# A 32-partition shift copied by ScalarE instead of loaded, and evictions shared 8 to 7, in the mixing stage of a long convolution

## The chip, the cores and the metric

The kernel runs on one core of one Trainium2 chip, in one launch. The metric is the device time of that launch in microseconds (us), as the median of several runs.

## The reference

The input `x` is (4, 512, 512, 16) in float32. Two layers are applied, each as a residual on a group-normalised input:

```python
x = x + _L0_conv_ref(_gn(x), h0, numerators, denumerator)   # long convolution through FFTs
x = x + _L1_conv_ref(_gn(x), kernel, bias, radius)          # 3x3 cosine-similarity convolution
```

Layer 0 builds a 512 x 512 impulse response for each of the 16 x 16 channel pairs, as a quotient of two small polynomials in the frequency plane, and convolves every channel with it:

```python
X = jnp.fft.rfft2(x, s=(2 * l1, 2 * l2), axes=(-3, -2))
Y = jnp.einsum('...hwi,ijhw->...hwj', X, H_full)
y = jnp.fft.irfft2(Y, s=(2 * l1, 2 * l2), axes=(-3, -2))[..., :l1, :l2, :]
```

Layer 1 divides a 3 x 3 convolution by norms of the input and the kernel, takes an arccosine, and gates with two tanh factors. The change is in layer 0, where `X` is multiplied by `H_full` and summed over the 16 input channels.

## The kernel before

The launch has four phases: the filter (`filter_phase`), the transform of the input along one image axis (`forward_phase`), the mixing (`conv_phase`), and the transform back with the whole of layer 1 (`last_phase`). They hand data on through tensors in HBM: `g_d` (filter), `x_d` (input), `y_d` (result).

`conv_phase` works through 513 rows, one for each frequency along the first axis. For one row, everything along the other axis is transformed, multiplied and transformed back in blocks. The steps of a row are spread over several turns of the loop, so that in turn n:

- `mix` multiplies row n. For each of 128 frequencies it takes the weights `gh` (128 values of contraction by 32) and the input `xe` and writes the PSUM tile `pm`, 32 partitions for each quarter of the frequencies. `pm` is evicted to `yf`, once in each of the four parts k = 0 to 3 of a turn. `pm` has two buffers.
- `g_part` transforms the filter of row n+1 (PSUM tiles `pg0` and `pg1`, three buffers in all) and evicts it to `gh`, two evictions in each part. The first `mix` of a row needs the whole `gh` of that row.
- `over_q` transposes `yf` of row n-1 into `pz`; ScalarE copies half of it to `zq`, and five VectorE operations form `z` from `zq` and `pz`.
- `x_part` (k=0) transforms the input of row n+2 into `px`, evicted in two halves to `xe[:, 0]`. `x_late` then multiplies this by phases on GpSimd (four `xu`, then two operations on `xl`), and GpSimd stores `xe[:, 0]` and `xl` to `xf_d`.
- `half_shift` and `load_xe` complete `xe`. `xe` holds eight copies t = 0 to 7 of the row, each shifted by 16 t partitions, where what runs out at the end is taken from `xl`. t = 4, a shift by 64 partitions, is made by two ScalarE copies of 64 partitions; the six others are loaded from `xf_d` by SP in the next turn.
- `turn_x` (k=2) makes the transform matrix of a row (`turn` on ScalarE, `dfs_n` on VectorE).
- `over_g` (k=2) transforms `z` of row n-2 back into `py`, evicted to `yo` and stored by GpSimd.

`px`, `pz` and `py` share three PSUM buffers. Fifteen evictions in a row go through one helper, `evict`: every third goes to VectorE (in the settled rows four `gh` and one `xe`), the rest to ScalarE (four `gh`, four `yf`, one `xe`, one `yo`). Its lines are 728 (VectorE) and 730 (ScalarE).

Each engine works through its instructions in one fixed order. That order is made when the program is built: a scheduler takes instructions from the Python program by priority as they become ready by its own model, so an instruction can stand ahead of others that come before it in the text. In the settled rows ScalarE's order is: `yf`, `gh`, `zq` of k=0; `xe`; half shift 0; `yf` of k=1; `turn`; `gh`, `zq` of k=1; half shift 1; `yf`, `gh`, `zq` of k=2; `yo`; `yf`, `gh`, `zq` of k=3. VectorE's is: `gh`, `z` of k=0; `xe`; `dfs_n`; `gh`, `z` of k=1, of k=2, of k=3.

Of the kernel before, what the change touches and what calls it, by code (L numbers as in the profile page):

```python
# [46 lines left out]
P = 128  # L47
N = 512
B = 4
C = 16  # L50
# [6 lines left out]
XF = F * 2 * B  # L57
XP = XF + 128
# [138 lines left out]
def dram(t, row, offset, *dims):  # L197

    pitch = t.shape[1]
    lead = [[pitch, t.shape[0]]] if row is None else []  # L200
    return bass.AP(tensor=t.tensor, offset=t.offset + (row or 0) * pitch + offset,
                   ap=lead + [list(d) for d in dims])
# [494 lines left out]
def conv_phase(tc, cst, g_d, x_d, y_d):  # L697
    nc = tc.nc
    with ExitStack() as ctx:
# [20 lines left out]
        rows = [(0, 0, 0), (0, 0, 1)] + [(n // P, n % P, None) for n in range(1, N)]  # L720
        n_rows = len(rows)
        state = {}
        flip = [0]

        def evict(dst, src):
            flip[0] += 1
            if flip[0] % 3 == 0:
                nc.vector.tensor_copy(dst, src)  # L728
            else:
                nc.scalar.copy(dst, src)  # L730

        def load_g(n):
            rc, r, plane = rows[n]
            g = io.tile([P, C, 8 * C], F32, name="g")
            t, w = g.rearrange("p j x -> p (j x)"), C * 8 * C
            if plane is None:
                nc.sync.dma_start(out=t, in_=dram(g_d[rc], r, 0, [w, P], [1, w]))
            else:
                for to, at in ((0, (0, 96)[plane]), (64, (64, 32)[plane])):
                    nc.sync.dma_start(out=t[to : to + 32], in_=dram(g_d[rc], r, at * w, [w, 32], [1, w]))  # L740
                    nc.gpsimd.memset(t[to + 32 : to + 64], 0.0)
            state["g", n] = g

        def load_x(n):
            rc, r, plane = rows[n]
            x = io.tile([P, B, 8 * C], F32, name="x")
            t, w = x.rearrange("p b x -> p (b x)"), B * 8 * C
            if plane is None:
                nc.sync.dma_start(out=t, in_=dram(x_d[rc], r, 0, [w, P], [1, w]))
            else:  # L750
                nc.gpsimd.memset(t[S:], 0.0)
                nc.sync.dma_start(out=t[:S], in_=dram(x_d[rc], r, plane * S * w, [w, S], [1, w]))
            state["x", n] = x
# [16 lines left out]
        def x_part(n, b):  # L770

            if b == 0:

                state["xe", n] = xep.tile([P, 8, F, 2, 2, 2], F32, name="xe")
            if b % 2 == 0:
                state["px"] = ps_f.tile([P, 2, F, 2], F32, name="px", tag="full")
            px = state["px"]
            nc.tensor.matmul(px[:, b % 2].rearrange("p f c -> p (f c)"), state["x", n][:, b],
                             state["dfs", n], start=True, stop=True)
            if b % 2:  # L780
                evict(state["xe", n][:, 0, :, b // 2], px.rearrange("p k f c -> p f c k"))
            if b == B - 1:
                del state["x", n], state["dfs", n]

# [22 lines left out]
        def half_shift(n, half):  # L807

            dst, src = ((slice(0, 64), state["xe", n][64:, 0]), (slice(64, P), state["xl"][:64]))[half]
            nc.scalar.copy(state["xe", n][dst, 4].rearrange("p f h c k -> p (f h c k)"),  # L810
                           src.rearrange("p f h c k -> p (f h c k)"))

        def load_xe(n):
            src = xf_d[n % 4]
            for t in (1, 5):
                nc.sync.dma_start(
                    out=state["xe", n][:, t : t + 3].rearrange("p t f h c k -> p t (f h c k)"),
                    in_=bass.AP(tensor=src.tensor, offset=src.offset + t * C * XP,
                                ap=[[XP, P], [C * XP, 3], [1, XF]]),
                )  # L820

        def g_part(n, j):


            if j % 4 == 0:
                state["pg"] = [ps_g.tile([P, 4, F], F32, name=f"pg{c}", tag="pg") for c in range(2)]
            g, pg = state["g", n], state["pg"]
            for c in range(2):
                half = slice(64 * c, 64 * c + 64)
                nc.tensor.matmul(pg[c][:, j % 4], g[half, j], dg[half], start=True, stop=True)  # L830
            if j == 3:
                state["gh", n] = ghp.tile([P, F, 2, C], F32, name="gh")
            if j % 4 == 3:
                for c in range(2):
                    evict(state["gh", n][:, :, c, j - 3 : j + 1], pg[c].rearrange("p j f -> p f j"))
            if j == C - 1:
                del state["g", n]

        def mix(n, g):

            if g % 8 == 0:
                state["pm"] = ps_m.tile([P, 8, 8, 2 * B], F32, name="pm")
            xe, gh, pm = state["xe", n], state["gh", n], state["pm"]
            for q in range(4):
                f = g + 32 * q
                nc.tensor.matmul(  # L846
                    pm[32 * q : 32 * q + 32, g % 8], gh[:, f].rearrange("p c j -> p (c j)"),
                    xe[:, :, f].rearrange("p t h c k -> p t (h c k)"), start=True, stop=True,
                )
            if g == 7:  # L850

                state["y", n] = yp.tile([P, 16, 32, 4], F32, name="yf")
            if g % 8 == 7:
                evict(state["y", n][:, :, g - 7 : g + 1].rearrange("p t g x -> p g t x"),
                      pm.rearrange("p g t (h x) -> p g (t h) x", h=2))
            if g == 31:
                del state["xe", n], state["gh", n]

# [30 lines left out]
        def over_g(n, k):  # L889

            rc, r, plane = rows[n]
            if k == 0:
                state["py"] = ps_f.tile([P, 2, 2, 8, C], F32, name="py", tag="full")
            z, d, py = state["z", n], state["zd", n], state["py"]
            odd, c2 = k // 2, k % 2
            for half in range(2):
                s0 = 2 * half + odd
                if s0 % 2 == 0:
                    zs = z[:, :, s0 + c2]
                elif s0 == 1:  # L900
                    zs = (d[:, :, 0], z[:, :, 5])[c2]
                else:
                    zs = (z[:, :, 4], d[:, :, 1])[c2]
                nc.tensor.matmul(
                    py[64 * half : 64 * half + 64, odd], ig[:, s0, c2],
                    zs.rearrange("p (t h) j -> p h t j", h=2),
                    start=(c2 == 0), stop=(c2 == 1),
                )
            if k < 3:
                return  # L910
            del state["z", n], state["zd", n]
            yo = yop.tile([P, 4 * P], F32, name="yo")
            evict(yo.rearrange("p (x j t) -> p x j t", x=4, j=C), py.rearrange("p o h t j -> p (o h) j t"))
            if plane is None:
                nc.gpsimd.dma_start(out=dram(y_d[rc], r, 0, [4 * P, P], [1, 4 * P]), in_=yo)  # L915
            else:
                for half in range(2):
                    nc.gpsimd.dma_start(
                        out=dram(y_d[rc], r, (64 * half + 32 * plane) * 4 * P, [4 * P, 32], [1, 4 * P]),
                        in_=yo[64 * half : 64 * half + 32],  # L920
                    )

        def step(n):


            def row(k):
                return 0 <= n + k < n_rows

            if row(3):
                load_x(n + 3)  # L930
            if row(2):
                load_g(n + 2)
            if row(1):
                load_xe(n + 1)
            for k in range(4):
                if row(0):
                    for g in range(8):
                        mix(n, 8 * k + g)
                if row(1):
                    for j in range(4):  # L940
                        g_part(n + 1, 4 * k + j)
                if row(-1):
                    for t in range(4):
                        over_q(n - 1, 4 * k + t)
                if row(2) and k == 0:
                    for m in range(B):
                        x_part(n + 2, m)
                    x_late(n + 2)
                if row(2) and k >= 2:
                    half_shift(n + 2, k - 2)  # L950
                if row(3) and k == 2:
                    turn_x(n + 3)
                if row(-2) and k == 2:
                    for m in range(4):
                        over_g(n - 2, m)
# [482 lines left out]
```

## Time and profile before

| | |
|---|---|
| median of 3 runs | 16582.36 us (16561.65 to 16588.23) |
| the profiled execution | 16601.06 us |
| its span, first to last instruction | 16599.1 us |
| TensorE clock granted, mean | 0.973 |
| rows of the mixing phase | 513, from 4767.9 to 13720.4 us by the last operation on `xl` |
| HBM traffic over the span | 272 GB/s; in the mixing phase about 325 |
| eviction of 128 x 512 on ScalarE, on VectorE | 592 ns (`yf`), 688 ns (`gh`) |
| half shift, 64 x 1024 | 1044 and 1051 ns |

The profile shows one execution. PE is TensorE, PEld its weight loads, DVE is VectorE, ACT ScalarE, POOL GpSimd, SP the engine that issues most of the transfers. A line such as `L730 ACT COPY yf<-pm` names the line of the kernel, the engine, the operation, and the tile written and read. In the views of waits, "A <- B: total, times, longest" says that instruction A stood idle until B ended, in us. In a timeline the first two columns are start and duration in us, and the brackets hold the idle time before it and what ended it. "issue" is idle time for which the profile shows no cause. A line of the table of windows has the length of the window, then busy time of PE, PEld, DVE, ACT and POOL, the granted clock, the share of time that the DMA engines were busy, and GB/s.

### The profile page before, as it was taken

To read this page: it belongs to the slowest core of one execution; us is meant where nothing else is said; L and a number is where in the kernel's file an instruction comes from. 1 tells how busy PE (TensorE), PEld (TensorE's weight loads), DVE (VectorE), ACT (ScalarE), POOL (GpSimd) and SP (SyncE) were. 2 spreads that over 40 slices of the span, in tenths; PEclk is the share of its full clock that TensorE was granted. 3 is DMA by queue.
4 is the path that set the end of the run, shared out by engine and by line. 5 is a ranking of instruction groups with operands and counts; after the bars stand their busy time and mean duration, and the time that the engine had idled before them with its cause. 6 is when DMAs were issued, how large, how long until landed. Compare 5 with 4: busy or idle time off the path is not lost. (4 is left out here: it accounts for less than half of the span.)

```text
span 16599.1 us, 545650 instructions
## 1 busy us (share of the span) xinstructions
PE 15057.2 (91%) x232588; PEld 11240.5 (68%) x232588; DVE 10596.9 (64%) x22299; ACT 9042.9 (54%) x18799; POOL 10362.7 (62%) x10669
## 2 busy tenths in 40 slices
PE   7999999998988899889899989898888888988888
PEld 5555555554557777777777777777777777767777
DVE  8999999993545555555555555555555552357877
ACT  5666666663345555555555555555555551027888
POOL 7777777772346666666666666666666660237766
PEclk7999999999999999999999999999999999989999
DMA  4888888878878888888888888888888886885531
GB/s 134 233 235 236 232 238 235 240 226 257 253 262 327 321 328 326 326 326 323 326 328 320 328 325 329 325 323 327 319 325 328 321 324 236 309 289 167 165 108 69
DMA packets 2914698, 4543.40 MB, mean 274 GB/s; under 512 B 126114, under 2 KB 2094460, under 8 KB 2801422
## 3 DMA queue, kind: packets, MB, share of 16 engines
q1 hardware_dynamic: 2703070, 3836.37, 67.4%
q0 software_dynamic: 172336, 605.00, 9.4%
q10 hardware_dynamic: 36864, 67.13, 1.2%
q8 instruction: 1833, 30.03, 0.7%
q14 instruction: 595, 4.87, 0.1%
HBM read 3030.71 MB, written 1477.31 MB: 272 GB/s over the span
## 5 line engine op out<-in xcount | busy, mean ns | idle before, releaser
L830 PE MATMUL pg<-c_dg,g 64*128 64x128 f32 x32832 | 2851.6, 290 | 372.2 <-ACT gh L730 220.5
L846 PE MATMUL pm<-xe,gh 128*32 128x64 f32 x131328 | 2370.2, 222 | 486.0 <-issue 234.5
L830 PEld LDWEIGHTS pg<-c_dg,g 64*128 64x128 f32 x32832 | 2293.3, 189 | 716.2 <-ACT gh L730 278.1
L846 PEld LDWEIGHTS pm<-xe,gh 128*32 128x32 f32 x131328 | 1998.2, 110 | 1072.6 <-issue 838.6
L875 DVE TENSOR_TENSOR z<-zq,pz 128x256 f32<-128x256 f32 x2052 | 859.4, 419 | 2695.4 <-ACT zq L874 2641.7
L728 DVE COPY gh<-pg 128x512 f32<-128x512 f32 x2046 | 1408.3, 688 | 1148.2 <-PE pg L830 1144.1
L450 PE MATMUL pt<-ev_in,c_todd 128*128 128x512 f32 x4096 | 1927.3, 609 | 109.0 <-ACT u L338 83.4
L799 POOL TENSOR_TENSOR xu<-xe,c_late 128x256 f32<-128x256 f32 x2052 | 1392.2, 702 | 845.6 <-ACT xe L730 826.7
L507 DVE RECIPROCAL dn<-dn 128x256 f32<-128x256 f32 x1024 | 1716.9, 1716 | 0.0
L730 ACT COPY yf<-pm 128x512 f32<-128x512 f32 x2046 | 1211.9, 592 | 901.5 <-PE pm L846 887.9
L382 POOL TENSOR_TENSOR sp<-m,dn 128x512 f32<-128x512 f32 x1024 | 1301.1, 1272 | 615.0 <-DVE dn L507 528.8
L810 ACT COPY xe<-xl 64x1024 f32<-64x1024 f32 x513 | 539.1, 1051 | 1892.1 <-POOL xl L801 1892.1
L450 PEld LDWEIGHTS pt<-ev_in,c_todd 128*128 128x128 f32 x4096 | 728.6, 190 | 1021.8 <-issue 704.3
L730 ACT COPY gh<-pg 128x512 f32<-128x512 f32 x2058 | 1201.2, 584 | 356.7 <-PE pg L830 355.1
L867 PE MATMUL pz<-c_ident,yf 128*128 128x128 f32 x8208 | 1365.6, 289 | 27.1 <-issue 14.1
L398 PEld LDWEIGHTS pg<-c_dinv,sp 64*128 64x128 f32 x16384 | 1004.5, 196 | 464.6 <-ACT sp L387 210.8
L409 ACT COPY st<-pg 128x256 f32<-128x256 f32 x2048 | 617.2, 391 | 1281.2 <-PE pg L398 1281.2
L801 POOL TENSOR_TENSOR xl<-xl,xu 128x1024 f32<-128x1024 f32 x513 | 1210.0, 2359 | 40.2
L398 PE MATMUL pg<-c_dinv,sp 64*128 64x128 f32 x16384 | 1106.7, 287 | 70.4 <-ACT sp L387 47.4
L1281 PE MATMUL pc<-l_band,xn 128*128 128x160 f32 (+2 forms) x6144 | 1078.0, 334 | 50.7 <-DVE e_o L1336 50.4
L883 POOL TENSOR_TENSOR zd<-z 128x512 f32<-128x512 f32 x513 | 653.6, 1274 | 742.4 <-DVE z L875 742.3
L915 POOL DMA_DIRECT2D y_d<-yo x511 | 296.5, 580 | 1305.0 <-ACT yo L730 1279.1
(211 smaller groups left out, 30874.7 us busy)
## 6 DMA issues: line engine op xcount, KB each, us to landing
xe<-xf_d SPq DMA_DIRECT2D x1026, 1536.0 KB
g<-g_d SPq DMA_DIRECT2D x511, 1024.0 KB
g_d<-st SPq DMA_DIRECT2D x256, 1024.0 KB
ev_in<-g_d SPq DMA_DIRECT2D x1024, 256.0 KB
g_d<-ot SPq DMA_DIRECT2D x1024, 256.0 KB
xf_d<-xe POOLq DMA_DIRECT2D x513, 448.0 KB, 8.2
xf_d<-xl POOLq DMA_DIRECT2D x513, 448.0 KB, 5.5
x_d<-xo SPq DMA_DIRECT2D x128, 1024.0 KB
```

The source lines that it names most:

```text
L382: nc.gpsimd.tensor_mul(w["sp"], w["m"], bc(w["dn"], 2, [P, 2, 2, P]))
L398: nc.tensor.matmul(pg[u][:, n, k].rearrange("p a x -> p (a x)"), w["sp"][q, k, c, :], dinv[q, 2 * kp + k, c, :], start=(c == 0), stop=(c = ...
L450: nc.tensor.matmul(pt, todd[:, c, kc, hh * P : hh * P + P], ev[:, kc, c], start=(kc == 0), stop=(kc == 1),)
L507: nc.vector.reciprocal(w["dn"], w["dn"])
L728: nc.vector.tensor_copy(dst, src)
L730: nc.scalar.copy(dst, src)
L799: nc.gpsimd.tensor_mul(u[:, :, h, c], xe[:, :, h, 1 - c], bc(late[:, 1 + c], 2, [P, F, 2]))
L801: nc.gpsimd.tensor_add(xl.rearrange("p f h c k -> p (f h c k)"), xl.rearrange("p f h c k -> p (f h c k)"), u.rearrange("p f h c k -> p (f ...
L830: nc.tensor.matmul(pg[c][:, j % 4], g[half, j], dg[half], start=True, stop=True)
L846: nc.tensor.matmul(pm[32 * q : 32 * q + 32, g % 8], gh[:, f].rearrange("p c j -> p (c j)"), xe[:, :, f].rearrange("p t h c k -> p t (h c k ...
L867: nc.tensor.transpose(pz[:, t % 4].rearrange("p v q x -> p (v q x)"), y[:, at].rearrange("p g x -> p (g x)"), ident)
L1281: nc.tensor.matmul(pc[:, lo:hi, :].rearrange("p w j -> p (w j)"), xns[q][:, h * P + dh : h * P + dh + P], bands[dh][:, o : o + hi - lo, :] ...
```

## The change

Three edits, all in `conv_phase`:

- Copy t = 2, a shift by 32 partitions, is made by four ScalarE copies of 32 partitions (`quarter_shift`): quarter 0 in part k=0, quarters 1 and 2 in k=1, quarter 3, which reads `xl`, in k=3 of the program's text.
- `load_xe` loads five copies: t = 1 and 3 in one transfer, 5 to 7 in the other.
- `evict` is told the engine: VectorE gets the second half of `xe`, `gh` of `pg1`, `yf` of k=1 and k=3, and `yo` (8 in a row); ScalarE gets 7.

```diff
-        flip = [0]
-
-        def evict(dst, src):
-            flip[0] += 1
-            if flip[0] % 3 == 0:
+
+        def evict(dst, src, vector):
+            if vector:
                 nc.vector.tensor_copy(dst, src)
             else:
                 nc.scalar.copy(dst, src)
...
-                evict(state["xe", n][:, 0, :, b // 2], px.rearrange("p k f c -> p f c k"))
+                evict(state["xe", n][:, 0, :, b // 2], px.rearrange("p k f c -> p f c k"), b == 3)
...
+        def quarter_shift(n, q):
+
+            src = state["xl"][:32] if q == 3 else state["xe", n][32 * q + 32 : 32 * q + 64, 0]
+            nc.scalar.copy(state["xe", n][32 * q : 32 * q + 32, 2].rearrange("p f h c k -> p (f h c k)"),
+                           src.rearrange("p f h c k -> p (f h c k)"))
+
         def load_xe(n):
             src = xf_d[n % 4]
-            for t in (1, 5):
+            for t in (slice(1, 4, 2), slice(5, 8)):
+                of = range(8)[t]
                 nc.sync.dma_start(
-                    out=state["xe", n][:, t : t + 3].rearrange("p t f h c k -> p t (f h c k)"),
-                    in_=bass.AP(tensor=src.tensor, offset=src.offset + t * C * XP,
-                                ap=[[XP, P], [C * XP, 3], [1, XF]]),
+                    out=state["xe", n][:, t].rearrange("p t f h c k -> p t (f h c k)"),
+                    in_=bass.AP(tensor=src.tensor, offset=src.offset + of[0] * C * XP,
+                                ap=[[XP, P], [of.step * C * XP, len(of)], [1, XF]]),
                 )
...
-                    evict(state["gh", n][:, :, c, j - 3 : j + 1], pg[c].rearrange("p j f -> p f j"))
+                    evict(state["gh", n][:, :, c, j - 3 : j + 1], pg[c].rearrange("p j f -> p f j"), c == 1)
...
-                      pm.rearrange("p g t (h x) -> p g (t h) x", h=2))
+                      pm.rearrange("p g t (h x) -> p g (t h) x", h=2), g % 16 == 15)
...
-            evict(yo.rearrange("p (x j t) -> p x j t", x=4, j=C), py.rearrange("p o h t j -> p (o h) j t"))
+            evict(yo.rearrange("p (x j t) -> p x j t", x=4, j=C), py.rearrange("p o h t j -> p (o h) j t"), True)
...
-                if row(2) and k >= 2:
-                    half_shift(n + 2, k - 2)
+                if row(2):
+                    for q in ([0], [1, 2], [], [3])[k]:
+                        quarter_shift(n + 2, q)
+                    if k >= 2:
+                        half_shift(n + 2, k - 2)
```

In the built program ScalarE's order in a settled row is: `yf`, `gh`, `zq` of k=0; `xe`; quarters 0, 1, 2; `gh`, `zq` of k=1; half shift 0; `yf` of k=2; quarter 3; `gh`, `zq` of k=2; half shift 1; `turn`; `gh`, `zq` of k=3. VectorE's is: `gh`, `z` of k=0; `xe`; `dfs_n`; `yf` of k=1; `gh`, `z` of k=1; `gh`, `z` of k=2; `yo`; `yf` of k=3; `gh`, `z` of k=3. On TensorE the first matmul into `pg0` and the first into `pg1` of the next row stand ahead of the first `mix` of a row; before, only the one into `pg0` did. On SP the two loads of `xe` come one after the other, then `g`, then `x`; before, `g` stood between the two.

## The prediction

> **What bounds the kernel now.** I read the page first, for the shares of the engines.
>
> ```profile
> PE 15057.2 (91%) x232588; PEld 11240.5 (68%) x232588; DVE 10596.9 (64%) x22299; ACT 9042.9 (54%) x18799; POOL 10362.7 (62%) x10669
> ```
>
> No engine is full over the whole span, so I went to the stage that is changed. The view of line 801 (the last step of the turned copy `xl`, once in each row) dates it: 513 rows, and (13720.4 - 4767.9) / 512 = 17.485 us a row. It also shows who waits for `xl`.
>
> ```profile
> L801 POOL TENSOR_TENSOR xl<-xl,xu x513: 2337/2360/2380, 4767.9 to 13720.4; 128x1024 f32<-128x1024 f32 x171
> ...
>   ACT xe L810: 1892.1, 513
> ```
>
> ScalarE stands 1892 / 513 = 3.7 us in every row before the half shift that reads `xl`. From the spacing of these 513 starts: 210 rows take 16.86 to 16.94 us, the median is 17.05, the tail runs to 23. Next the waits of the stage, from 4820 to 13700 us:
>
> ```profile
> DVE z L875 <- ACT zq L874: 2617.2, 1556, 6.7
> ACT xe L810 <- POOL xl L801: 1866.4, 507, 6.5
> ...
> PE pm L846 <- issue: 232.7, 259, 3.2
> PE pg L830 <- ACT gh L730: 214.5, 238, 3.8
> PE pg L830 <- issue: 144.7, 96, 2.9
> PE pm L846 <- DMA xe<-xf_d: 82.2, 73, 3.0
> ```
>
> TensorE's waits are small and spread; ScalarE and VectorE show the long regular ones. So I took one quiet row (`pm` starts at 7056.77 and again at 7073.83) from the timelines of ScalarE, VectorE and TensorE:
>
> ```profile
> 7064.96 0.38 ACT L874 COPY zq<-pz 128x256 f32<-128x256 f32 x1
> 7069.08 1.06 ACT L810 COPY xe<-xl 64x1024 f32<-64x1024 f32 x1 [3.75 <-POOL xl L801]
> 7070.16 0.59 ACT L730 COPY yf<-pm 128x512 f32<-128x512 f32 x1
> 7070.64 0.59 ACT L730 COPY gh<-pg 128x512 f32<-128x512 f32 x1
> 7071.12 0.39 ACT L874 COPY zq<-pz 128x256 f32<-128x256 f32 x1
> ```
>
> ```profile
> 7071.54 0.42 DVE L875 TENSOR_TENSOR z<-zq,pz 128x256 f32<-128x256 f32 x1 [3.98 <-ACT zq L874]
> ...
> 7073.05 0.68 DVE L728 COPY gh<-pg 128x512 f32<-128x512 f32 x1
> ```
>
> ```profile
> 7071.28 1.16 PE L830 MATMUL pg<-c_dg,g 64*128 64x128 f32 x14 [1.10 <-ACT gh L730]
> ...
> 7073.83 1.10 PE L846 MATMUL pm<-xe,gh 128*32 128x64 f32 x64 [0.39 <-ACT zq L874]
> ```
>
> The row is a loop of latencies. Counted from `pm`: `px` starts at 2.61, its evictions let GpSimd start `xu` at 4.34, `xl` ends at 12.27, the half shift ends at 13.4, then come `yf`, `gh` and `zq` on ScalarE, the five VectorE operations on `z`, and only behind them VectorE's last `gh`, which ends at 7073.73; `pm` of the next row starts 0.10 later. That wait is labelled `zq`, but `zq` had ended at 7073.48; `gh` is the last thing that `pm` needs. TensorE's own work in the row is 17.06 - 1.10 - 0.39 = 15.57 us.
>
> DMA is the near second: in the same row
>
> ```profile
> 7056.70:7073.80 17.10, 15.57 (x360) 12.55 (x360) 9.57 (x27) 9.25 (x17) 11.29 (x11) 1.00 0.89 333
> ```
>
> 333 GB/s at a share of 0.89, and 82 us of TensorE's waits are for `xe` loads.
>
> [...]`yf`, whose matmuls ended at 7065.02, sat behind the half shift until 7070.16. So the order of instructions on each engine is what must be costed. [...]the 64-partition half shifts took 1044 and 1051, so a 32-partition copy is taken at 1.04 us. [...]the quiet rows here stay at 333 to 336.
>
> **The change, part by part**, per row, with the order that the changed program has on each engine.
>
> 1. Loads. `xe` by five shifts, 2 + 3, instead of 3 + 3: 2560 KB for 3072. The row's traffic falls from 5504 KB (5.64 MB: `xe` 3072, `g` 1024, `x` 256, stores 896 + 256) to 4992 KB (5.11 MB), at 335 GB/s from 16.8 to 15.3 us. SP now issues both `xe` loads ahead of `g`; `g` lands later by the second `xe` load (1.57 MB, about 5 us), but is wanted only at the end of the row; `x` stays last. This gives back the waits for `xe`: 82 / 513 = 0.16 us a row, and no more, since the clean row does not end on a load.
>
> 2. Four quarter copies on ScalarE, 4 x 1.04 = +4.2 us; three evictions leave it (2 `yf`, 1 `yo`, 0.59 each, -1.8). ScalarE's work goes from 9.25 to about 11.6 us. Quarters 0 to 2 follow the `xe` eviction: they wait for VectorE's `xe` (5.5), run to about 8.6, and hold back `gh` and `zq` of k=1 and the first half shift to about 10.4 and `yf` of k=2 to 10.9. They hide in the 3.75 us that ScalarE idled: 1.2 us are left before `xl` ends. Without that cover each would cost 0.95 us.
>
> 3. Quarter 3 takes the half shift's place as the first reader of `xl`: same moment, same 1.04 us. Behind it come `gh` and `zq` of k=2, then the second half shift, the turn, and `gh`, `zq` of k=3. `yf` of k=2 is now ahead of the wait: -0.48 us on the chain (7070.16 to 7070.64 is the step between queued copies).
>
> 4. VectorE gets `yo` and two `yf`, loses none: 3 x 0.69 us more, 9.6 to 11.6 us. But in its queue `yo` and `yf` of k=3 stand between the operations on `z` of k=2 and the last `gh`. Those operations wait for the late `zq`; so both evictions, ready long before, run after it and ahead of the `gh` that `pm` needs. Step between queued VectorE copies: 0.60 us (7055.99 to 7056.59). +1.20 on the chain. The third, `yf` of k=1, runs at about 6.0, ahead of its waits: nothing.
>
> 5. On TensorE both first `pg` matmuls of the next row now precede `pm`, where one did. 12 instructions rather than 14 lie between `pm` and `pz`, at 1.08 / 14 = 0.078 us: -0.16. They wait for ScalarE's `gh` of k=3, done at about 16.1, before VectorE's at 17.4: nothing.
>
> 6. GpSimd: same order, same steps. Its start depends on ScalarE's `xe` eviction, which still comes before the quarters; `y_d` now waits for VectorE's `yo`, at 16.2, ahead of any use.
>
> Sum for a clean row: 16.90 - 0.16 - 0.48 + 1.20 = 17.46 us.
>
> Then the tail. TensorE is also interrupted by itself ("issue": 232.7 + 144.7 + 28 for `py` + 14 for `pz` = 420 us, 0.82 a row), partly absorbed by its slack. I took 506 rows of TensorE's timeline: row length less waits for other engines is TensorE's own time (mean 16.6, one row in ten over 18.4). The larger of this and of the chain (moved by a late `px`), averaged over the rows, is 17.34 for a chain of 16.90; with 0.16 for late loads this gives 17.50, against 17.485 measured. For a chain of 17.46 it is 17.82, without late loads. So (17.82 - 17.485) x 513 = +172 us. The profiled execution took 16601 (span 16599) and would take about 16773; the three runs' median is 19 us lower, so **16754 us**.
>
> Unknowns, both ends: interruptions may shrink with lighter DMA traffic (all gone: 17.46, -13 us) or, falling before `px` where no slack absorbs them, stay in full (17.46 + 0.43 = 17.89, +208). The chain may be 0.16 shorter (17.30: 17.68, +100) or longer (base 17.06 rather than 16.90, 17.62: 17.96, +244). I take the middle.
>
> **Rivals.**
> - Faster: the loads set the row. For it: 333 GB/s, rows that end on `xe` loads, and the changed kernel moves 9% less. If loads were the only limit, the row could fall to TensorE's 15.57 plus its interruptions 0.82 = 16.4: -1.09 x 513 = -560 us, 16020. It decides if VectorE's last `gh` ends before the loads land, that is if the chain grows by less than nothing. Against: quiet rows end 0.10 us after that `gh`, and only 73 of 513 rows name a load. 8%.
> - No change: the chain grows, but the interruptions nearly vanish with the traffic; 17.46 to 17.55, 16570 to 16615. Nothing shows that they come from traffic: in one disturbed row (7003.5 to 7023) the granted clock was 0.91. 9%.
> - Slower still: ScalarE's queue, now with 1.2 us before `xl`, fills, and the quarters push the chain. From 1.45 us per quarter on it decides; with a chain longer by 0.5 and the tail in full it is 17.46 + 0.5 + 0.4: +450 us, 17030.[...] 8%.
> - The change does not do what it says: excluded, the built program has 2 + 3 shifts and 8 to 7 evictions in each row.
>
> **The numbers.** Likeliest (75%): +70 to +290, 16650 to 16870, at 16754. The range for 8 in 10 takes in most of the no-change case below and the edge of the slower one: 16590 to 16880. A measurement here can tell about 0.2%, 33 us. Faster by more: the loads' 8% and 3 of the no-change case's 9, 11%. Within: the other 6, and 2 of the likeliest, 8%. Slower: 73 + 8 = 81%.
>
> **What would show it.** Right: `pm` of the next row waits about 1.5 to 2 us, ending 0.1 us after VectorE's `gh`, which follows `yo` and `yf` at steps of 0.60; ScalarE's wait for `xl` at about 1.2 us in front of a 32-partition copy of 1.04; waits for `xe` loads near zero at about 290 GB/s; quiet rows at 17.46. Wrong: quiet rows under 17.0, or `pm` released by a load or by ScalarE; or ScalarE no longer idle before `xl`.

## The result and the profile after

The changed kernel takes 16753.72 us (median of 4 runs, 16742.82 to 16783.95) where the kernel before takes 16585.29 (4 runs, 16561.65 to 16590.23). The ratio is 1.0108, with a 95% interval of 1.0093 to 1.0122: slower by 168 us. The forecast was 16754.

The profiled execution took 16752.71 us, its span is 16750.6, and the mean granted clock is 0.97 as before. First the page's line of engine shares, after the change:

```profile
PE 15075.3 (90%) x232588; PEld 11194.9 (67%) x232588; DVE 11532.3 (69%) x23838; ACT 10422.9 (62%) x19312; POOL 10361.8 (62%) x10669
```

ScalarE and VectorE have more to do, by 1380 and 935 us. No engine is full. Then the view of the last step of `xl`, whose line is now 799:

```profile
L799 POOL TENSOR_TENSOR xl<-xl,xu x513: 2339/2367/2460, 4765.5 to 13865.1; 128x1024 f32<-128x1024 f32 x171
...
  ACT xe L814: 460.4, 485
```

A row takes (13865.1 - 4765.5) / 512 = 17.773 us, 0.288 more than before; times 513 that is 148 of the span's 151 us. So the loss lies in the mixing phase, and in every row of it. ScalarE now waits for `xl` 460 us in all instead of 1892, and the reader is the 32-partition copy. The waits of the phase, from 4820 to 13850 us, say who waits now (total, times, longest):

```profile
DVE z L880 <- ACT zq L879: 2168.9, 1567, 5.0
...
PE pm L851 <- issue: 474.8, 406, 4.0
ACT xe L814 <- POOL xl L799: 452.8, 480, 3.7
...
PE pm L851 <- DVE gh L726: 278.9, 370, 1.3
...
PE pg L835 <- issue: 146.8, 120, 3.0
```

TensorE's waits for `xe` loads are gone from the list. In their place stand two things: `pm` waits for VectorE's `gh` in 370 rows, and TensorE's idle time without a cause in this view ("issue") has grown. Summed over `pm`, `pg`, `py`, `pz` and `px` it is 688 us, 1.35 a row, where it was 0.83. I call these stretches interruptions of TensorE.

One quiet row shows the queues: `pm` starts at 7064.08 and again at 7081.45. Its lines from the timelines of ScalarE, VectorE and TensorE (start, duration, idle time before and what ended it):

```profile
7073.15 0.38 ACT L879 COPY zq<-pz 128x256 f32<-128x256 f32 x1
...
7074.51 0.57 ACT L728 COPY yf<-pm 128x512 f32<-128x512 f32 x1
7076.05 1.05 ACT L814 COPY xe<-xl 32x1024 f32<-32x1024 f32 x1 [0.97 <-POOL xl L799]
7077.12 0.58 ACT L728 COPY gh<-pg 128x512 f32<-128x512 f32 x1
7077.60 0.38 ACT L879 COPY zq<-pz 128x256 f32<-128x256 f32 x1
```

```profile
7078.01 0.42 DVE L880 TENSOR_TENSOR z<-zq,pz 128x256 f32<-128x256 f32 x1 [2.26 <-ACT zq L879]
...
7079.52 0.68 DVE L726 COPY yo<-py 128x512 f32<-128x512 f32 x1
7080.12 0.68 DVE L726 COPY yf<-pm 128x512 f32<-128x512 f32 x1
7080.72 0.68 DVE L726 COPY gh<-pg 128x512 f32<-128x512 f32 x1
```

```profile
7064.08 1.10 PE L851 MATMUL pm<-xe,gh 128*32 128x64 f32 x64 [0.86 <-DVE gh L726]
...
7066.48 1.89 PE L776 MATMUL px<-dfs_n,x 128*128 128x256 f32 x8
...
7078.27 0.42 PE L851 MATMUL pm<-xe,gh 128*32 128x64 f32 x13 [1.52 <-issue]
...
7081.45 1.10 PE L851 MATMUL pm<-xe,gh 128*32 128x64 f32 x64 [0.51 <-DVE gh L726]
```

The chain reads from top to bottom: ScalarE stands 0.97 us for `xl`; quarter 3, `gh` and `zq` follow at once; `zq` lets VectorE form `z`; behind that come `yo` and `yf`, at steps of 0.60, and only then the `gh` that `pm` needs. It ends at 7081.40, `pm` starts at 7081.45. TensorE was interrupted for 1.52 us in this row, and still waited 0.51 us for `gh` at its end: the row takes 17.37, so the slack took the interruption up. Of 512 rows, 332 take 17.3 to 17.4 us. The table of windows shows DMA at a share of 0.79 and 290 GB/s from 5000 to 13500 us, where it was 0.87 and 325.

### The profile page after: what moved, and what is told of

It is laid out like the page before. It is cut to its first block, busy times and chain, and to the rows that moved or that the text cites. A ratio compares the mean times of both kernels' runs of the same rounds, so it can differ in the third digit from the quotient of the medians.

```text
span 16750.6 us, 547682 instructions
## 1 busy us (share of the span) xinstructions
PE 15075.3 (90%) x232588; PEld 11194.9 (67%) x232588; DVE 11532.3 (69%) x23838; ACT 10422.9 (62%) x19312; POOL 10361.8 (62%) x10669
## 5 line engine op out<-in xcount | busy, mean ns | idle before, releaser
L851 PE MATMUL pm<-xe,gh 128*32 128x64 f32 x131328 | 2414.7, 222 | 766.4 <-issue 482.3
L835 PE MATMUL pg<-c_dg,g 64*128 64x128 f32 x32832 | 2783.1, 292 | 224.6 <-issue 150.7
L835 PEld LDWEIGHTS pg<-c_dg,g 64*128 64x128 f32 x32832 | 2220.7, 189 | 573.1 <-issue 241.4
L814 ACT COPY xe<-xe 32x1024 f32<-32x1024 f32 x1539 | 1611.6, 1047 | 717.4 <-DVE xe L726 705.2
L728 ACT COPY yf<-pm 128x512 f32<-128x512 f32 x1026 | 595.1, 580 | 1016.2 <-PE pm L851 1015.9
L909 PE MATMUL py<-z,c_ig 128*64 128x256 f32 x6156 | 1068.9, 409 | 31.1 <-issue 28.1
```

The costliest lines, as they stand in the source:

```text
L814: nc.scalar.copy(state["xe", n][32 * q : 32 * q + 32, 2].rearrange("p f h c k -> p (f h c k)"), src.rearrange("p f h c k -> p (f h c k)"))
L851: nc.tensor.matmul(pm[32 * q : 32 * q + 32, g % 8], gh[:, f].rearrange("p c j -> p (c j)"), xe[:, :, f].rearrange("p t h c k -> p t (h c k ...
```

## The experiments

My theory: in a quiet row the order of instructions on ScalarE and VectorE sets the time (the loop through `xl`), and what is over it comes from interruptions of TensorE. The rivals: the loads of `xe` set the row; or the copies do, by filling ScalarE. Every kernel was measured against the kernel before on the same chip. "Quiet" is the commonest row length, to about 0.02; the mean is the spacing of all 513 `xl` starts; "idle" is TensorE's idle time of cause "issue" per row.

| | ratio to before, 95% interval | median, us | mean row | quiet row | idle |
|---|---|---|---|---|---|
| before | 1 | 16585 | 17.49 | 16.90 | 0.83 |
| changed kernel | 1.0108 (1.0093 to 1.0122) | 16754 | 17.77 | 17.33 | 1.35 |
| e1, sharing alone | 1.0218 (1.0201 to 1.0236) | 16955 | 18.19 | 17.82 | 0.96 |
| e2, shift alone | 1.0149 (1.0131 to 1.0167) | 16845 | 17.90 | 17.17 | 1.48 |
| e3, one load less | 1.0044 (1.0033 to 1.0054) | 16665 | 17.61 | 16.89 | 1.40 |
| e4, `yo` back to ScalarE | 1.0093 (1.0073 to 1.0113) | 16752 | 17.79 | 16.88 | 1.63 |
| e5, no `xe` loads | 0.9852 (0.9838 to 0.9867) | 16343 | 16.98 | 16.95 | 0.29 |
| e6, order of loads | 1.0004 (0.9995 to 1.0013) | 16599 | 17.46 | 16.90 | 0.88 |
| e7, copies of `xl` last | 0.9848 (0.9826 to 0.9871) | 16328 | 16.93 | 15.73 | 1.13 |
| e8, half shift 1 last | 1.0002 (0.9993 to 1.001) | 16590 | 17.41 | spread | 0.89 |
| e9, e3 with loads late | 1.1207 (1.1189 to 1.1226) | 18576 | 21.3 | | 0.21 |
| e10, e7 with loads late | 1.1212 (1.1196 to 1.1229) | 18596 | 21.4 | | 0.26 |

**e1: the sharing alone.** The changed kernel with six loads and the two half shifts of before.

```diff
-                if row(2):
-                    for q in ([0], [1, 2], [], [3])[k]:
-                        quarter_shift(n + 2, q)
-                    if k >= 2:
-                        half_shift(n + 2, k - 2)
+                if row(2) and k >= 2:
+                    half_shift(n + 2, k - 2)
...
-            for t in (slice(1, 4, 2), slice(5, 8)):
+            for t in (1, 5):
```

> Eviction sharing alone: 8 on VectorE and 7 on ScalarE as in the changed kernel, with six shifts loaded and two half shifts as before. Chain theory: the half shift still waits for xl, with yf, gh and zq of k=2 behind it; VectorE has yo and yf of k=3 between z of k=2 and the last gh, 2 x 0.60 us more. Quiet rows 16.90 + 1.20 = 18.1 (within 0.15), mean row near 18.3, so 16585 + 0.8 x 513 = about 17000. Rival, the loads set the row: traffic is that of before, so the time is that of before within 40 us.

Measured: 16954.85 us, and a quiet row of 17.82. Against the changed kernel that is 0.49 more. What differs on the chain is `yf` of k=2, which here still stands behind the wait for `xl`; the prediction priced that at 0.48. Against before, 0.92 more, and I had expected 1.20 for the two evictions on VectorE. By the times of the changed kernel's quiet row, 0.21 of the difference is the earlier `px` (2.40 us after `pm` here too) and 0.05 the earlier start of `pm` behind `gh`; I had left both out.

**e2: the shift alone.** Quarter copies and five loads, with evictions by every third as before.

```diff
+        def quarter_shift(n, q):
+            src = state["xl"][:32] if q == 3 else state["xe", n][32 * q + 32 : 32 * q + 64, 0]
...
-            for t in (1, 5):
+            for t in (slice(1, 4, 2), slice(5, 8)):
...
-                if row(2) and k >= 2:
-                    half_shift(n + 2, k - 2)
+                if row(2):
+                    for q in ([0], [1, 2], [], [3])[k]:
+                        quarter_shift(n + 2, q)
+                    if k >= 2:
+                        half_shift(n + 2, k - 2)
```

> Quarter copies and five loads alone, evictions as before (every third on VectorE). Chain theory: quarter 3 waits for xl, then gh, zq of k=2, half shift 1, turn, yo, yf and gh of k=3 all on ScalarE; that gh ends about 17.1 after pm and releases the next pm. Quiet rows 17.15, ended by ScalarE and not by VectorE, mean 17.6: about +50 us on before, 16640. Rival, the loads set the row: 9 percent less traffic, up to 560 us less, 16020.

Measured: 16844.84 us. The quiet row was 17.17, as expected, and it ended on ScalarE's `gh`; but the mean row is 17.90, and the idle time 1.48 a row. The mechanism of the quiet row held, the forecast of the tail failed: I had let the interruptions stay as they were. The two parts do not add up: 370 us and 260 us alone, 168 us together. In a quiet row each relieves what the other loads: the new sharing takes three evictions from ScalarE, which the quarters fill, and the quarters put `yf` of k=2 ahead of the wait for `xl`.

**e3: one load less, and nothing in its place.** The kernel before, without the load of copy t = 2; three fixed `xe` buffers hold zeros there. So it leaves out a seventh of the shifted copies that are not t = 0.

```diff
+                if n < 3:
+                    fixed[n] = xep.tile([P, 8, F, 2, 2, 2], F32, name=f"xe{n}")
+                    nc.gpsimd.memset(fixed[n][:, 2], 0.0)
+                state["xe", n] = fixed[n % 3]
...
-            for t in (1, 5):
+            for t in (slice(1, 4, 2), slice(5, 8)):
```

> The kernel before with copy t=2 neither loaded nor copied (filled with zeros once, in three fixed buffers of xe, so the output leaves this copy out). Nothing else differs on ScalarE and VectorE; SP issues g after both xe loads. Chain theory: quiet rows stay at 16.9; only the waits for xe loads go, 0.16 us a row: -80 us, 16500. Rival, the loads set the row: down to 16.4 a row, -560 us, 16020. Halfway (-250 or more) would mean that traffic costs more than the waits named after it.

Measured: 16665.39 us over 12 runs, slower by 0.44%. The quiet row stayed at 16.89, so the loads do not set it. But less traffic, at no price on any engine, made the program slower: the idle time of TensorE rose from 0.83 to 1.40 a row. This was the largest surprise, and it says that my tail was wrong in its cause.

**e4: `yo` back to ScalarE.**

```diff
-            evict(yo.rearrange("p (x j t) -> p x j t", x=4, j=C), py.rearrange("p o h t j -> p (o h) j t"), True)
+            evict(yo.rearrange("p (x j t) -> p x j t", x=4, j=C), py.rearrange("p o h t j -> p (o h) j t"), False)
```

> The changed kernel with the eviction of yo back on ScalarE, where it stands after the turn and ahead of gh of k=3. Chain theory: one step of 0.60 less ahead of VectorE's last gh: quiet rows 17.35 - 0.60 = 16.75, mean 17.3, -250 us on the changed kernel: 16500, 85 below before. Rival, ScalarE or VectorE is full (their busy time sets the row): moving 0.6 us from one to the other changes nothing beyond 50 us: 16750. Loads: traffic as in the changed kernel, 16750.

Measured: 16751.71 us, no better, although the quiet row fell by 0.45, to 16.88. It did not fall by the whole step of 0.60, because `yo` on ScalarE stands ahead of `gh` of k=3, and the first matmul into `pg1` waits for that. From e4's timelines of ScalarE and TensorE:

```profile
7067.45 0.57 ACT L728 COPY yo<-py 128x512 f32<-128x512 f32 x1
7067.91 0.59 ACT L728 COPY gh<-pg 128x512 f32<-128x512 f32 x1
```

```profile
7068.55 0.48 PE L835 MATMUL pg<-c_dg,g 64*128 64x128 f32 x2 [0.67 <-ACT gh L728]
```

And the gain of the quiet rows was taken by idle time: 1.63 a row. A shorter chain leaves less slack for interruptions to hide in; that they also grew is not explained by it.

**e5: no loads of `xe` at all.** The kernel before; the six copies hold zeros, written once.

```diff
+                    nc.gpsimd.memset(fixed[n][:, 1:4], 0.0)
+                    nc.gpsimd.memset(fixed[n][:, 5:], 0.0)
...
-            if row(1):
-                load_xe(n + 1)
```

> The kernel before without any load of xe (the six copies are filled with zeros once, so the output leaves them out); stores, g and x as before: 2432 KB a row instead of 5504. The question is TensorE's idle time without a named cause (0.82 us a row before, 1.41 in the kernel with one load less). Theory F, it is instructions of TensorE fetched late because their transfers stand among the bursts of loads: it falls under 0.3 us a row, quiet rows stay at 16.9 by the chain, mean near 17.1: -200 us, 16380. Rival C, the clock or power limit interrupts TensorE: it stays at 0.8 or more and the mean at 17.4: 16540.

Measured: 16342.84 us. The waits of e5, from 4850 to 13500 us:

```profile
PE pm L851 <- DVE gh L729: 204.2, 471, 0.4
...
PE pm L851 <- issue: 126.2, 149, 1.4
```

`pm` waits for VectorE's `gh` in nearly every row, rows take 16.95 (95% under 17.04), and the idle time falls to 0.29 a row. Of the two theories put down before the run, that of late instructions had named under 0.3 and that of the clock 0.8 or more. DMA moves 149 GB/s there instead of 325. Two things follow. The chain of queues alone gives 16.9 us, with or without loads. And nearly all that a row takes above it comes with the traffic of the `xe` loads: as waits for them, or as interruptions of TensorE.

**e6: the order of the loads.** The kernel before, with both `xe` loads ahead of `g` on SP, as in the changed kernel. It asks whether that order makes the interruptions.

```diff
+        order = InOrder(tc, nc.sync)
...
-            if row(2):
-                load_g(n + 2)
-            if row(1):
-                load_xe(n + 1)
+            with order:
+                if row(1):
+                    load_xe(n + 1)
+                if row(2):
+                    load_g(n + 2)
```

> The kernel before with six shifts loaded as before, but both loads of xe issued ahead of g on SP, as the changed kernel does. Traffic, ScalarE and VectorE as before. If the order of the loads makes the longer interruptions of the kernel with one load less: 1.2 us or more a row without cause, mean 17.6, 16650. If their start in the row does (the store of xl lands earlier with less traffic, which this kernel does not change): 0.8 to 0.9, 16585 within 40.

Measured: 16598.95 us over 12 runs, ratio 1.0004; idle 0.88. With six loads, the order is not it.

**e7: the copies that read `xl` put last.** The changed kernel; quarter 3 and half shift 1 of a row go behind `zq` of k=3 on ScalarE, where `xl` has long been ready. Nothing else changes.

```diff
+        order = InOrder(tc, nc.scalar)
...
-                if row(-1):
-                    for t in range(4):
-                        over_q(n - 1, 4 * k + t)
+                with order:
+                    if row(-1):
+                        for t in range(4):
+                            over_q(n - 1, 4 * k + t)
+                    if row(2) and k == 3:
+                        quarter_shift(n + 2, 3)
+                        half_shift(n + 2, 1)
...
-                    for q in ([0], [1, 2], [], [3])[k]:
+                    for q in ([0], [1, 2], [], [])[k]:
```

> The changed kernel with the two ScalarE copies that read xl put behind zq of k=3, so that nothing of the row waits for xl on ScalarE. Chain theory alone: the loop through xl is gone, z of k=2 ends at about 13.8 and VectorE's last gh at 15.7, so quiet rows are TensorE's own, 15.6 to 15.8, and with interruptions as assumed in the prediction the mean is 16.75, 16200. With the interruptions found since (1.35 to 1.6 us a row, none of them absorbed): 15.7 + 1.5 = 17.2, 16440. Rival, POOL's xl is not what ScalarE's wait costs: 16750.

Measured: 16328.07 us, faster than both kernels: 263 us under the runs of before beside it (16590.95), some 426 under the changed kernel's median, and between the two sums put down before the run (16200 and 16440). Quiet rows take 15.73 us; TensorE's own work in a row was 15.57. ScalarE's timeline in e7:

```profile
7082.89 0.58 ACT L729 COPY gh<-pg 128x512 f32<-128x512 f32 x1 [2.86 <-PE pg L836]
7083.65 0.37 ACT L880 COPY zq<-pz 128x256 f32<-128x256 f32 x1 [0.18 <-DVE gh L727]
7084.05 1.05 ACT L815 COPY xe<-xl 32x1024 f32<-32x1024 f32 x1
7085.11 1.04 ACT L809 COPY xe<-xl 64x1024 f32<-64x1024 f32 x1
```

The copies run without a wait, and ScalarE waits for TensorE instead. So the loop through `xl` cost 17.33 - 15.73 = 1.60 us in a quiet row of the changed kernel. The mean row gained only 0.84, since interruptions stay (1.13 a row) and now stand in the open.

**e8: the same on the kernel before.** Half shift 1 behind `zq` of k=3; six loads and old sharing.

```diff
+                    if row(2) and k == 3:
+                        half_shift(n + 2, 1)
...
-                if row(2) and k >= 2:
-                    half_shift(n + 2, k - 2)
+                if row(2) and k == 2:
+                    half_shift(n + 2, 0)
```

> The kernel before with its second half shift put behind zq of k=3 on ScalarE: six shifts loaded, evictions as before. Chain theory: the loop through xl is gone here too, but the row's 5.64 MB then set it, at 335 GB/s 16.8 us, with waits for xe loads of 0.5 us and more a row: mean 17.2 to 17.4, 16440 to 16540. If it falls as far as the changed kernel with the same edit, loads do not bound it.

Measured: 16590.11 us over 12 runs, ratio 1.0002: nothing gained, against my expectation. Its waits, from 4850 to 13500 us:

```profile
PE pm L847 <- DMA xe<-xf_d: 328.7, 181, 5.2
PE pm L847 <- issue: 271.6, 266, 2.7
```

The regular wait for `gh` is gone, and waits for the loads of `xe` have taken its place, 329 us where the kernel before shows 81; DMA is at 326 GB/s, as before. With six loads the traffic is the next limit, right behind the loop. In e7, with five, no wait of TensorE for `xe` loads is left. So the two parts of the change, with five loads and the new sharing, carry a gain that only shows once the loop is cut; how much of the 262 us between e7 and e8 is the load and how much the sharing, these two runs do not separate.

**e9 and e10: the loads started later.** What sets the interruptions? Before the change the first `xe` load is issued 2.8 us ahead of ScalarE's eviction of `px`, in e3, e4 and the changed kernel 4.6 to 5.1 ahead. To start the loads later I put SP's load of `x`, now for one row further on and waiting for `px` to free its buffer, ahead of them: e9 on e3 (the same part left out), e10 on e7.

```diff
+        in_turn = InOrder(tc, nc.sync)
...
-            if row(3):
-                load_x(n + 3)
-            if row(2):
-                load_g(n + 2)
-            if row(1):
-                load_xe(n + 1)
+            with in_turn:
+                if row(4):
+                    load_x(n + 4)
+                if row(1):
+                    load_xe(n + 1)
+                if row(2):
+                    load_g(n + 2)
```

> The kernel with one load less (copy t=2 filled with zeros once and left out of the output), with SP's order changed: the load of x that waits for px stands ahead of the two loads of xe, so that the burst of loads starts about 4.4 us after pm instead of 1.0 us before it. On VectorE the eviction of px moves ahead of the last two operations on z of k=0; all else as in the kernel with one load less. Start theory: TensorE's idle time without cause depends on where in the row the burst stands; the share that falls 2 us after px (0.37 of 1.41 us a row) goes, in all 0.8 to 1.0, mean 17.3: about 16500. Rival, amount theory: the time for which the transfers are busy sets it, 1.4 as without the edit, 16665.

> The changed kernel with the copies of xl last (16328 us) and in addition the burst of loads started at px, as in the run beside it. Start theory: idle time without cause from 1.13 to 0.8 or 0.9 a row, nearly all of it on the path since quiet rows are TensorE's own 15.7: 130 us less, 16200. Amount theory: 16330. If g, now landing last, is late: waits of pg for g, 16400 and more.

Measured: 18575.54 and 18595.89 us, 12% slower. SP's queue waits in e10 from 5000 to 13000 us, and TensorE's in e9 from 4850 to 13500:

```profile
SPq L749 <- PE px L778: 7138.2, 375, 21.9
```

```profile
PE pg L836 <- DMA g<-g_d: 938.8, 402, 3.0
...
PE pm L852 <- DMA xe<-xf_d: 161.5, 177, 2.5
```

SP stands 7138 / 375 = 19 us in every row for `px`, with the loads of `xe` and `g` behind it in its queue; `g` is wanted by the next `pg`, and that precedes the next `px`. I had closed a new loop of 21 us. The idle time fell to 0.21 and 0.26, but in rows about 4 us longer, so this does not answer the question. Both expectations failed, and so did the attempt.

## Why the prediction was right

The time was met, and the chain was read rightly. The tail was right in sum only: two errors nearly cancel, and that the forecast fits to within 1 us is luck.

- **Loads (part 1).** Right: waits for `xe` went from 82 us to none, at 290 GB/s as forecast. Right also that quiet rows do not end on loads: e3 and e5 leave them at 16.89 and 16.95. The rival in which loads set the row falls with these two.
- **Quarter copies (part 2).** A copy takes 1047 ns, for the 1.04 us taken from the half shifts (1044 and 1051), and quarters 0 to 2 end 8.57 us after `pm`, for 8.6 forecast. What ScalarE has behind them ends 0.1 later than forecast and `xl` almost 0.2 earlier, so 0.97 us were left before `xl`, not 1.2. Three queued copies took 3.17 us, 1.06 each, where I had priced one without cover at 0.95 (in the quiet row of before, the step from the first half shift to the eviction behind it, 7062.52 to 7063.47). The cover was enough, and it counted: in e2, with the old sharing, ScalarE waits for `xl` 132 us in all, in 353 rows, and the kernel is slower by 260 us. The rival of the full ScalarE queue is real, but in e2, not here.
- **`yf` of k=2 ahead of the wait (part 3).** -0.48 forecast; e1 against the changed kernel gives 0.49.
- **`yo` and `yf` ahead of the last `gh` (part 4).** +1.20 forecast; the timeline shows two steps of 0.60. The line that I took the step from before the change has an operation on `z` behind the eviction, not a second eviction; the step between two evictions came out the same. Undoing one (e4) gave 0.45 back, with ScalarE's `gh` next in line.
- **`pg` ahead of `pm` (part 5).** -0.16 forecast; `px` starts 2.40 after `pm` instead of 2.61, -0.21. And `pm` follows `gh` by 0.05, not 0.10.
- **Sum for a clean row.** 17.46 forecast, 17.33 to 17.37 measured: too long by about 0.1.
- **The tail.** Here the step that failed: I kept the interruptions at 0.82 a row, though the change moves the loads, and let the longer chain absorb more of them, 0.36 a row left over. They rose to 1.35; the slack took up much of it, and (17.77 - 17.33) = 0.44 was left over. Too small by 0.08. With the clean row the errors are -0.1 and +0.08 in a row, and in the span 151 us measured for 172 forecast; the medians, 168 us apart, stand nearer to the forecast than the profiled pair does.
- **The rival of no change** said that interruptions nearly vanish with lighter traffic, against which I wrote that nothing shows that they come from traffic. e5 shows that they do come with the `xe` loads: 0.29 a row without them. But one load less gives more of them, not fewer (e3). The way the rival went was wrong, and so was my argument against it. In the disturbed row that I named, the clock is 1.00 until TensorE resumes at 7014.80, after an interruption of 2.60 us, and 0.79 from there on. The low clock comes behind the interruption and cannot be its cause:

```profile
7003.50:7014.80 11.30, 8.66 (x240) 7.33 (x241) 6.75 (x19) 4.92 (x9) 9.26 (x9) 1.00 0.84 307
7014.80:7023.00 8.20, 8.20 (x120) 5.72 (x119) 2.87 (x7) 4.41 (x8) 2.00 (x3) 0.79 0.77 292
```

The traces do show what the interruptions are. Among the DMA transfers of before is a queue of instructions (packets, MB, share):

```profile
q8 instruction: 1833, 30.03, 0.7%
```

Every packet has 16 KiB. TensorE's stream in the same trace has 469,406 records (232,588 matmuls, as many weight loads, 4230 semaphore and drain instructions), 256.1 to a packet; so I take these packets for blocks of TensorE's own instructions. From 4850 to 13400 us TensorE is interrupted 389 times for over 0.15 us before the change and 559 times after it. Every one of these stretches ends 0.9 to 1.7 us after a block has landed, 1.40 in the median, and all of them stand at the same place in the blocks, 193 to 195 instructions past a multiple of 256 in TensorE's stream. In the quiet row above, the view of DMA from 7075.8 to 7076.6 us has this block (packets, MB, share):

```profile
q8 instruction: 1, 0.02, 7.2%
```

It landed at 7076.87, and `pm` resumed at 7078.27. From this fixed place and these times I read that TensorE stood waiting for its next instructions. Of the blocks, 28% came late in this sense before the change, 41% after it, 43% in e3 and 14% in e5. Moving one takes the same 0.95 to 0.96 us, in the median, in all four. What differs is when it starts to move: more than 3.5 us after TensorE began the block before it (counted from the place where the stretches end), in 41% of the cases before, 51% after, 51% in e3 and 10% in e5. That goes with full DMA engines, as far as before and after show. Taken over the 2 us from 0.5 us after TensorE began the block before, a busy share under 0.6 leaves 3% of the blocks late before the change and 7% after it; a share over 0.8 makes it 37% and 60%.

What stays open is why more blocks start late under lighter `xe` traffic. The order of the loads alone, with six of them, is excluded (e6). Their place in the row stays a suspect: in the kernel before, the first 3 us of the row carry 154 GB/s at a DMA share of 0.56, after the change 339 at 0.96. The tables of windows for the two quiet rows, from `pm` on, first before and then after (length, then the busy times of PE, PEld, DVE, ACT, POOL, the clock, DMA share, GB/s):

```profile
7056.77:7059.77 3.00, 3.00 (x84) 2.76 (x85) 1.99 (x6) 1.31 (x3) 2.55 (x2) 1.00 0.56 154
7059.77:7071.77 12.00, 10.90 (x265) 8.57 (x266) 5.58 (x15) 6.27 (x12) 8.17 (x8) 1.00 1.01 389
```

```profile
7064.08:7067.08 3.00, 3.00 (x83) 2.73 (x84) 2.03 (x6) 1.52 (x3) 2.54 (x2) 1.00 0.96 339
7067.08:7079.08 12.00, 10.48 (x262) 8.11 (x263) 6.92 (x18) 9.09 (x14) 8.16 (x8) 1.00 0.89 337
```

But e1 starts its loads as early (5.0 us ahead) and has an idle time of only 0.96, in longer rows; and e9 and e10 did not settle it.

## What to carry to other kernels

When work is handed from one engine to another, cost its place in the receiving queue, not its share of the engine: VectorE was 64% busy, and two evictions that stood between a late operation and the last one that TensorE needs still cost their full 0.60 us each in a quiet row. Look for the instruction that waits in the middle of a queue, here the copy that reads `xl`, and move it behind what does not need it: that was worth 1.6 us of a quiet row, while the copies themselves cost little there (15.73 us against TensorE's own 15.57). And keep the next limit in view: a change that loses alone can let another edit pay (e7 against e8). When TensorE idles without a cause in the view of waits, set its idle stretches beside the transfers of its instructions: here all 559 after the change stood at the same place in the blocks.

## What the runs showed of the hardware

- ScalarE and VectorE kept to one order: from 4850 to 13500 us, ScalarE's 17 operations of a row came in the same order in all 493 rows before the change, and its 18 in all 485 after it; so did VectorE's 26 and 29. In the quiet row of after, an operation that was ready did not pass one that waited: the last matmul into `py` ended at 7075.86, and its eviction `yo` started at 7079.52, behind the `z` that stood for `zq` until 7078.01.
- The idle time that the view of waits calls "issue" was, in this stage, TensorE waiting for a block of its instructions: so for each of the 389 stretches before, 559 after, 588 in e3 and 201 in e5. That is the reading above; what was measured before and after the change is that each ended 0.9 to 1.7 us after a block had landed. Before the change, 72% of the blocks came with no such stretch; the 28% that came late cost 0.83 us a row, and the 41% after the change 1.35.
- This idle time goes with the DMA traffic beside it, though not with the mean rate: 0.29 us a row at 149 GB/s (e5), 0.83 at 325 before the change, 1.35 at 290 after it. e5 also has the higher granted clock in this phase, 1.00 to 0.99.
- A mean of 333 GB/s was no ceiling for a burst: the row of before moves 389 GB/s for 12 us, after 3 us at 154. I had read the mean of the quiet rows as the limit (335 in the median of 198 of them). Yet e8, at a mean of 326, did wait for its loads.
- Three 32 x 1024 copies on ScalarE, queued one behind the other, took 3.17 us, 1.06 each, with no overlap (7069.48 to 7072.65 in the quiet row of after); two queued evictions of 128 x 512 from PSUM, of 0.59 us each, started 0.48 apart (7070.16 and 7070.64 in that of before). What makes the difference, no run here shows.
